# A relational graph convolution: comparison constants in a PSUM bank, and one bank for projections and placement

## The chip, the cores and the metric

The kernel runs on one core of a Trainium2 chip. A core has five engines with a queue each: TensorE (PE in the profile; PEld is its weight load), VectorE (DVE), ScalarE (ACT), GpSimd (POOL) and SyncE (SP). They share the on-chip memory SBUF. TensorE's results land in PSUM, which has 8 banks of 512 float32 columns on each of 128 partitions. The metric is device microseconds of the run, as a median of several runs. One further execution is recorded by the profiler, and all views of the profile are of that one.

## The reference

There are 12500 nodes with 128 features and 200000 edges (src to dst), sorted by dst. An edge's type is the place of the greatest of ten of its attributes. Each layer takes, for every node and type, the mean of the features of the edges' sources, multiplies it by the type's matrix and adds the node's own features times a root matrix and a bias. There are two layers, a relu after the first; then the input is added and each row normalized.

```python
def _rgcn_layer(x, src, dst, edge_type, w_rel, root, bias):
    seg = dst * NUM_REL + edge_type
    sums = segment_sum(x[src], seg); cnt = segment_sum(ones, seg)
    mean = (sums / maximum(cnt, 1.0)[:, None]).reshape(N, NUM_REL, -1)
    return einsum('nrd,rdo->no', mean, w_rel) + x @ root + bias
edge_type = argmax(msg[:, 16:-16], axis=1)
h = relu(_rgcn_layer(x, src, dst, edge_type, w_rel1, root1, b1))
out = layernorm(x + _rgcn_layer(h, src, dst, edge_type, w_rel2, root2, b2))
```

## The kernel before

The edges are cut into 1563 tiles of 128, one edge on each partition, and eight tiles make a group (`G`), 196 groups in a layer. The last group has three tiles. A tile's edges, sorted by destination, reach at most 12 nodes (`WN`), so a pair of type and node within a tile is one of 120 columns (`KW`).

**Preparation** runs by chunks of 128 tiles. `types(c)` loads attributes in two halves and calls `argmax` (L208 to L215): the greatest of ten values (L210), a comparison of all ten with it (L212), a product with descending ranks `riota` (L213), the greatest of these (L214), and the type from it (L215). `count(c)` counts the edges with equal key, and takes a key's neighbours from SBUF and the key itself from a PSUM copy (L309). Both write key, weight and source row per edge (`keyE`, `wE`, `idxE`), via TensorE transposes (L126, L127). Two chunks are prepared ahead of the loop, the others in steps between groups of the first layer.

**The layer loop** takes a group through four stages:

1. `gather` (L404): eight indirect DMAs on GpSimd's queue, each for 128 source rows of 128 float32. The buffers are a ring of 13 groups. All 3126 gathers of the two layers stand on this one queue.
2. `sums`: for each tile, DVE compares the column numbers `iota` with the edge's key and multiplies by its weight (L415, tile `oh`, 128 x 120); once per group it compares `iota` with `place` (L418, tile `at`). TensorE multiplies the rows by `oh` into `zp`, two banks (L421).
3. `project`: ACT copies `zp` to SBUF as `zs` (L436), ten TensorE products with the types' matrices are summed in `po` (L440), and ACT copies that to SBUF as `ms` (L443).
4. `add`: TensorE places `ms` by `at` into 80 node columns (`pa`, L451), and DVE adds these to `acc` (L458).

The loop is software-pipelined: while group g is gathered and summed, g-1 is projected and g-2 added. The order on each engine is made by a scheduler from the dependences, not written by hand. Where a stretch of nodes is complete, `hidden` or `final` finishes its rows (L345 to L395), in pieces of four 128-row tiles.

**PSUM before:** `ps_f` two banks (transposes, counts, root products), `ps_z` two buffers of two banks (`zp`), `ps_o` one bank (`po`), `ps_a` one bank (`pa`). A second path for unusual graphs stands behind a flag (from L551 on) and does not run with these inputs; it calls `argmax` too.

Of the kernel before, what the change touches and what calls it, by code (L numbers as in the profile page):

```python
# [9 lines left out]
F32 = mybir.dt.float32  # L10
# [3 lines left out]
ALU = mybir.AluOpType  # L14
AX = mybir.AxisListType
PSUM = bass.MemoryType.PSUM
# [4 lines left out]
P = 128  # L21
NREL = 10
EMB = 16
RS = 32
WN = 12
KW = NREL * WN
G = 8
QB = 4
SW = 80
# [4 lines left out]
YB = 512  # L34
W = 128
GT = 125
# [5 lines left out]
def rgcn_resnorm_kernel(ctx: ExitStack, tc: tile.TileContext, x, src, dst, attr, w_rel1, root1, b1,  # L42
# [14 lines left out]
    nc = tc.nc  # L57
    N, C = x.shape
    E = src.shape[0]
    D = attr.shape[1]  # L60
# [4 lines left out]
    GR = G * WN  # L65
# [17 lines left out]
    fin = ctx.enter_context(tc.tile_pool(name="fin", bufs=1))  # L83
    small = ctx.enter_context(tc.tile_pool(name="small", bufs=2))
    ps_f = ctx.enter_context(tc.tile_pool(name="ps_f", bufs=2, space=PSUM))

    hD = dram.tile([N, C], F32, name="hD")
    KD = dram.tile([1, L + NT * P + L], F32, name="KD")
# [2 lines left out]
    fast = ctx.enter_context(ExitStack())  # L91
    keep = fast.enter_context(tc.tile_pool(name="keep", bufs=1))
    prep = fast.enter_context(tc.tile_pool(name="prep", bufs=1))
# [4 lines left out]
    spool = fast.enter_context(tc.tile_pool(name="spool", bufs=3))  # L98
    ps_z = fast.enter_context(tc.tile_pool(name="ps_z", bufs=2, space=PSUM))
    ps_o = fast.enter_context(tc.tile_pool(name="ps_o", bufs=1, space=PSUM))  # L100
    ps_a = fast.enter_context(tc.tile_pool(name="ps_a", bufs=1, space=PSUM))

    ident = const.tile([P, P], F32, name="ident")
    make_identity(nc, ident)
# [1 line left out]
    keyE = keep.tile([P, NCH * CT], F32, name="keyE")  # L106
    wE = keep.tile([P, NCH * CT], F32, name="wE")
# [31 lines left out]
    iota = const.tile([P, W], F32, name="iota")  # L139
# [21 lines left out]
                   allow_small_or_imprecise_dtypes=True)  # L161
    riota = const.tile([P, NREL], F32, name="riota")
    nc.vector.tensor_scalar(riota, iota[:, :NREL], -1.0, float(NREL), op0=ALU.mult, op1=ALU.add)
    identb = const.tile([P, P], BF16, name="identb")
    nc.vector.tensor_copy(identb, ident)
    eps = const.tile([P, 1], F32, name="eps")
# [21 lines left out]
    place = keep.tile([GR, NCH * CT // G], F32, name="place")  # L188
# [15 lines left out]
            nc.scalar.dma_start(t, bi.rearrange("(c o) -> c o", o=1))  # L204
            bsb.append(t)

    def argmax(ty, v, p, n, pool):

        top = pool.tile([P, n], F32, name="top")
        nc.vector.tensor_reduce(top[:p], v, axis=AX.X, op=ALU.max)  # L210
        eq = pool.tile([P, n, NREL], F32, name="eq")
        nc.vector.tensor_tensor(eq[:p], v, top[:p, :, None].to_broadcast([p, n, NREL]), op=ALU.is_equal)  # L212
        nc.vector.tensor_tensor(eq[:p], eq[:p], riota[:p, None, :].to_broadcast([p, n, NREL]), op=ALU.mult)  # L213
        nc.vector.tensor_reduce(top[:p], eq[:p], axis=AX.X, op=ALU.max)  # L214
        nc.vector.tensor_scalar(ty, top[:p], -1.0, float(NREL), op0=ALU.mult, op1=ALU.add)  # L215

    def types(c):

        p = chunk_rows(c)
# [27 lines left out]
        for o in (0, H):  # L247
            m = prep.tile([P, H * D], F32, name="m")
            nc.sync.dma_start(m[:n], bass.AP(attr.tensor, attr.offset + (c * CE + o) * D, [[P * D, n], [1, H * D]]))
            if last:  # L250
                nc.sync.dma_start(m[n:p], bass.AP(attr.tensor, attr.offset + (E - P + o) * D,
                                                  [[P * D, 1], [1, H * D]]))
            argmax(ty[:p, o:o + H], m[:p].rearrange("p (j d) -> p j d", d=D)[:, :, EMB:EMB + NREL], p, H, prep)
            yield
        g0 = c * CT // G
        nc.vector.tensor_scalar(bt[:, g0:g0 + ng], bt[:, g0:g0 + ng], 0, N - 1, op0=ALU.max, op1=ALU.min)
# [152 lines left out]
    def sums(table, t0, n):  # L409

        g, gathers = gather(table, t0, n)
        oh = dpool.tile([P, G, KW], F32, name="oh")
        for j in range(n):
            t = t0 + j
            nc.vector.tensor_scalar(oh[:, j, :], iota[:, :KW], keyE[:, t:t + 1], wE[:, t:t + 1], op0=ALU.is_equal,  # L415
                                    op1=ALU.mult)
        at = spool.tile([GR, SW], F32, name="at")
        nc.vector.tensor_scalar(at, iota[:GR, :SW], place[:, t0 // G:t0 // G + 1], None, op0=ALU.is_equal)  # L418
        zp = ps_z.tile([P, G // QB, YB], F32, name="zp")
        for j in reversed(range(n)):  # L420
            m = nc.tensor.matmul(zp[:, j // QB, j % QB * KW:(j % QB + 1) * KW], g[:, j, :], oh[:, j, :],  # L421
                                 start=True, stop=True)
            if j < n - 1:
                tc.keep_in_program_order(m)
                continue

            for d in gathers[:j]:
                tc.add_manual_dep(m.ins, d.ins.name, whole, reason="one wait per group")
        return zp, at

    def project(l, n, zp):

        zs = zpool.tile([P, NREL, G, WN], F32, name="zs")
        for b in range(-(-n // QB)):
            m = min(QB, n - b * QB)
            nc.scalar.activation(zs[:, :, b * QB:b * QB + m, :],  # L436
                                 zp[:, b, :m * KW].rearrange("c (j r n) -> c r j n", r=NREL, n=WN), AF.Copy)
        po = ps_o.tile([P, C], F32, name="po")
        for r in range(NREL):
            nc.tensor.matmul(po[:n * WN], zs[:, r, :n].rearrange("c j n -> c (j n)"), wsb[l][:, r, :],  # L440
                             start=(r == 0), stop=(r == NREL - 1))
        ms = spool.tile([GR, C], F32, name="ms")
        nc.scalar.activation(ms[:n * WN], po[:n * WN], AF.Copy)  # L443
        return ms
# [2 lines left out]

    def add(t0, n, ms, at):

        pa = ps_a.tile([P, SW], F32, name="pa")  # L450
        nc.tensor.matmul(pa, ms[:n * WN], at[:n * WN], start=True, stop=True)  # L451
        if not offs:
            g0 = t0 // G
            offs.extend(nc.values_load_multi_w_load_instructions(
                bt[0:1, g0:min(NG, g0 + 4)], engines=[DVE], min_val=0, max_val=N - 1,
                skip_runtime_bounds_check_because=HELD)[1])
        s = ds(offs.pop(0), SW)
        nc.vector.tensor_tensor(acc[:, s], acc[:, s], pa, op=ALU.add)  # L458
# [90 lines left out]
    def each_tile(before, stages):  # L549

        with tc.For_i(0, E, GT) as e:  # L551
            d_i = gp.tile([P, 1], I32, name="gd_i")
            nc.sync.dma_start(d_i[:GT], dst[ds(e, GT)].rearrange("(e o) -> e o", o=1))
            a = gp.tile([P, 1, D], F32, name="ga")
            nc.sync.dma_start(a[:GT, 0], attr[ds(e, GT), :])
            ty = gp.tile([P, 1], F32, name="gty")
            nc.vector.memset(ty, 0.0)
            argmax(ty[:GT], a[:GT, :, EMB:EMB + NREL], GT, 1, gp)
            d = gp.tile([P, 1], F32, name="gd")
            mx = gp.tile([P, 2], F32, name="gmx")  # L560
            nc.vector.memset(d, -1.0)
            nc.vector.memset(mx[:, 1:2], -float(FAR))
            nc.vector.tensor_copy(d[:GT], d_i[:GT])
            nc.vector.tensor_copy(mx[:, 0:1], d)
            nc.vector.tensor_scalar(mx[:GT, 1:2], d[:GT], -1.0, None, op0=ALU.mult)
            gm = gp.tile([P, 2], F32, name="gm")
            nc.gpsimd.partition_all_reduce(gm, mx, P, bass_isa.ReduceOp.max)
            base = gp.tile([P, 1], F32, name="gbase")
            nc.vector.tensor_scalar(base, gm[:, 1:2], -1.0, 0.0, op0=ALU.mult, op1=ALU.max)
            nc.vector.tensor_scalar(base, base, float(N - 1), None, op0=ALU.min)  # L570
            bw = gp.tile([P, 2], I32, name="gbw")
            nc.vector.tensor_copy(bw[:, 0:1], base)
            nc.vector.tensor_tensor(d, d, base, op=ALU.subtract)
            span = gp.tile([P, 1], F32, name="gspan")
            nc.vector.tensor_tensor(span, gm[:, 0:1], base, op=ALU.subtract)
            nc.vector.tensor_scalar(span, span, 0.0, float(N - 1), op0=ALU.max, op1=ALU.min)
            nc.vector.tensor_copy(bw[:, 1:2], span)
            nc.vector.tensor_scalar(bw[:, 1:2], bw[:, 1:2], 7, None, op0=ALU.arith_shift_right)
            nc.vector.tensor_scalar(bw[:, 1:2], bw[:, 1:2], 1.0, None, op0=ALU.add)
            state = before(e, ty)  # L580
            nw = nc.values_load(bw[0:1, 1:2], min_val=1, max_val=-(-N // W), skip_runtime_bounds_check_because=HELD)
            b0 = nc.values_load(bw[0:1, 0:1], engines=[DVE, SP], min_val=0, max_val=N - 1,
                                skip_runtime_bounds_check_because=HELD)
            for body, after in stages:
                dw = gp.tile([P, 1], F32, name="gdw")
                nc.vector.tensor_copy(dw, d)
                with tc.For_i(0, nw, 1) as k:
                    body(dw, state, window(b0, k))
                    nc.vector.tensor_scalar(dw, dw, -float(W), None, op0=ALU.add)
                if after:  # L590
                    state = after(state)
# [101 lines left out]
```

## Time and profile before

| | us |
|---|---|
| median of 3 runs | 4721.93 (4706.83 to 4728.79) |
| profiled execution | 4026.78 |
| its span, first to last instruction | 4025.1 |
| GpSimd busy | 3023.0 |
| TensorE busy | 2499.6 |
| VectorE busy | 1345.0 |
| ScalarE busy | 566.0 |
| mean granted TensorE clock | 0.82 of full |

A row of the page's list of groups names line, engine, operation and tiles (out<-in), how often it ran, its busy time and mean duration, and then how long the engine stood idle just before it, with what ended most of that. In the chain of waits, "issue" is time in which an engine waited for nothing that the profile shows. A timeline row is a start, a duration, the engine and its instructions, merged where they follow each other. The profiled execution is 695 us shorter than the median of the runs.

### The profile page before, as it was taken

The numbers are of one execution on the slowest core, as the hardware profiler recorded it, in microseconds if no ns is written. First come the engines' busy times: TensorE is split into PE (matmuls) and PEld (weight loads), VectorE is DVE, ScalarE is ACT, GpSimd is POOL, SyncE is SP. The second block draws the span as 40 slices with busy tenths as digits, with TensorE's granted clock in tenths as the row PEclk, the third lists the DMA queues.
The fourth block names the chain that finished last, engine by engine and source line by source line (L and its number), as shares of the span: only waits on it lengthen the run. The fifth ranks groups of instructions, "written<-read, shape, count | busy, mean of one in ns | idle before, by whom it ended". The sixth has DMA issues, their size and how long they took to land.

```text
span 4025.1 us, 45940 instructions
## 1 busy us (share of the span) xinstructions
PE 2499.6 (62%) x16184; PEld 2382.6 (59%) x16184; DVE 1345.0 (33%) x4911; ACT 566.0 (14%) x1293; POOL 3023.0 (75%) x3142
## 2 busy tenths in 40 slices
PE   3666665656666666666555656666656666666666
PEld 2656565656556566655555656566656656665665
DVE  7443343334334333322222322223222322232222
ACT  0111111111111111111111111111111111111111
POOL 7777777777777777777767777777777777777775
PEclk9887888887888888788878887877888888878878
DMA  5332233233222222222222222222222222222222
GB/s 175 119 94 76 73 88 87 64 87 86 59 64 64 59 58 58 63 58 58 56 59 57 65 61 60 60 61 68 61 60 61 68 61 60 61 68 60 60 61 56
DMA packets 180736, 279.13 MB, mean 69 GB/s; under 512 B 55793, under 2 KB 127360, under 8 KB 177376
## 3 DMA queue, kind: packets, MB, share of 16 engines
q0 software_dynamic: 100032, 205.07, 20.2%
q1 hardware_dynamic: 77302, 69.59, 5.5%
q8 instruction: 136, 2.23, 0.2%
q10 hardware_dynamic: 3168, 1.44, 0.1%
q14 instruction: 98, 0.80, 0.1%
HBM read 262.28 MB, written 13.60 MB: 69 GB/s over the span
## 4 chain that ended last, share of the span: by engine, by line
POOL 61%; issue 28%; PE 6%; DMA 5%; DVE 0%; ACT 0%; POOLq 0%; ACTq 0%
POOL g L404 61%; DMA g<-in_x_dram,idxE 2%; PE zp L421 2%; DMA g<-hD,idxE 2%; PE po L440 2%; PE pf L355 1%; PE pf L356 1%; PE pf L350 0%; PE pa L451 0%; DVE acc L506 0%; DMA s_i<-in_src_dram 0%; DMA hD<-hb 0%; ACT ms L443 0%; POOLq L404 0%; DVE acc L458 0%
## 5 line engine op out<-in xcount | busy, mean ns | idle before, releaser
L421 PE MATMUL zp<-oh,g 128*128 128x120 f32 x6252 | 1207.7, 373 | 1445.8 <-DMA g<-in_x_dram,idxE 700.3
L421 PEld LDWEIGHTS zp<-oh,g 128*128 128x128 f32 x6252 | 1126.3, 279 | 1530.9 <-issue 1512.7
L404 POOL DMA_INDIRECT g<-in_x_dram,idxE x1563 | 1521.9, 974 | 482.4 <-issue 464.5
L404 POOL DMA_INDIRECT g<-hD,idxE x1563 | 1498.9, 959 | 495.5 <-issue 464.7
L415 DVE TENSOR_SCALAR oh<-iota,keyE,wE 128x120 f32<-128x120 f32 x3126 | 858.6, 346 | 1905.3 <-PE zp L421 1905.2
L440 PE MATMUL po<-w,zs 128*96 128x128 f32 x7840 | 1068.8, 297 | 0.6 <-ACT zs L436 0.6
L440 PEld LDWEIGHTS po<-w,zs 128*96 128x96 f32 x7840 | 1018.7, 185 | 1.5 <-ACT zs L436 0.9
L436 ACT ACTIVATE zs<-zp 128x480 f32<-128x480 f32 (+1 forms) x782 | 403.4, 567 | 2599.8 <-PE zp L421 2576.7
L458 DVE TENSOR_TENSOR acc<-acc,pa 128x80 f32 x392 | 93.0, 237 | 651.1 <-PE pa L451 641.0
L443 ACT ACTIVATE ms<-po 96x128 f32<-96x128 f32 x392 | 106.9, 273 | 703.5 <-PE po L440 703.2
L451 PE MATMUL pa<-at,ms 96*128 96x80 f32 (+1 forms) x784 | 184.2, 329 | 1.6 <-ACT ms L443 1.4
L451 PEld LDWEIGHTS pa<-at,ms 96*128 96x128 f32 (+1 forms) x784 | 172.9, 271 | 2.8 <-ACT ms L443 2.8
L418 DVE TENSOR_SCALAR at<-iota,place 96x80 f32<-96x80 f32 x392 | 107.1, 273 | 0.0
L309 DVE TENSOR_TENSOR eqb<-pf,kh 128x1344 bf16<-128x1344 f32 (+1 forms) x65 | 100.2, 1549 | 14.5 <-PE pf L313 13.9
L355 PE MATMUL pf<-root,fT 128*128 128x128 f32 x392 | 79.2, 284 | 0.7 <-DMA g<-hD,idxE 0.7
L356 PE MATMUL pf<-ident,a 128*128 128x128 f32 x392 | 76.1, 276 | 0.4 <-DVE a L345 0.4
L355 PEld LDWEIGHTS pf<-root,fT 128*128 128x128 f32 x392 | 59.6, 192 | 5.3 <-ACT fT L352 4.7
L356 PEld LDWEIGHTS pf<-ident,a 128*128 128x128 f32 x392 | 59.4, 192 | 1.3 <-DVE a L345 1.0
L311 PE MATMUL pf<-eqb,identb 128*128 128x512 bf16 (+1 forms) x130 | 50.0, 384 | 16.4 <-DVE eqb L309 16.4
L313 PE MATMUL pf<-eqb,identb 128*128 128x512 bf16 (+1 forms) x130 | 50.2, 386 | 0.0
L352 ACT ACTIVATE fT<-pf 128x512 f32<-128x512 f32 (+2 forms) x52 | 29.9, 575 | 11.3 <-PE pf L350 6.6
L313 PEld LDWEIGHTS <-identb 128*128 128x128 bf16 (+1 forms) x130 | 12.7, 97 | 26.6 <-issue 18.4
(96 smaller groups left out, 462.7 us busy)
## 6 DMA issues: line engine op xcount, KB each, us to landing
m<-in_edge_attr_dram SPq DMA_DIRECT2D x24, 1344.0 KB
g<-in_x_dram,idxE POOLq DMA_INDIRECT x1563
g<-hD,idxE POOLq DMA_INDIRECT x1563
xb<-in_x_dram SPq DMA_DIRECT2D x48, 256.0 KB
hD<-hb SPq DMA_DIRECT2D x24, 256.0 KB
hb<-hD SPq DMA_DIRECT2D x24, 256.0 KB
out_dram<-o SPq DMA_DIRECT2D x24, 256.0 KB
w<-in_L_gnn_w_rel_dram ACTq DMA_DIRECT2D x2, 640.0 KB
```

The source lines that it names most:

```text
L309: nc.vector.tensor_tensor(eq[:p], kp[:p, None, :R].to_broadcast([p, DB, R]), ahead, op=ALU.is_equal)
L355: nc.tensor.matmul(pr[:h, t, :], fT[:, t * P:t * P + h], rsb[l], start=True, stop=False)
L356: nc.tensor.matmul(pr[:h, t, :], a[:, t * P:t * P + h], ident, start=False, stop=True)
L404: return g, [nc.gpsimd.indirect_dma_start(out=g[:, j, :], out_offset=None, in_=table, in_offset=(bass.IndirectOffsetOnAxis(ap=idxE[:, t0 + ...
L415: nc.vector.tensor_scalar(oh[:, j, :], iota[:, :KW], keyE[:, t:t + 1], wE[:, t:t + 1], op0=ALU.is_equal, op1=ALU.mult)
L418: nc.vector.tensor_scalar(at, iota[:GR, :SW], place[:, t0 // G:t0 // G + 1], None, op0=ALU.is_equal)
L421: m = nc.tensor.matmul(zp[:, j // QB, j % QB * KW:(j % QB + 1) * KW], g[:, j, :], oh[:, j, :], start=True, stop=True)
L436: nc.scalar.activation(zs[:, :, b * QB:b * QB + m, :], zp[:, b, :m * KW].rearrange("c (j r n) -> c r j n", r=NREL, n=WN), AF.Copy)
L440: nc.tensor.matmul(po[:n * WN], zs[:, r, :n].rearrange("c j n -> c (j n)"), wsb[l][:, r, :], start=(r == 0), stop=(r == NREL - 1))
L443: nc.scalar.activation(ms[:n * WN], po[:n * WN], AF.Copy)
L451: nc.tensor.matmul(pa, ms[:n * WN], at[:n * WN], start=True, stop=True)
L458: nc.vector.tensor_tensor(acc[:, s], acc[:, s], pa, op=ALU.add)
```

## The change

A new pool `ps_c` holds one PSUM bank for the whole kernel. Into it go a copy of the column numbers (`iotaP`, 120 columns), a copy of the ranks (`riotaP`) and two places of 64 columns for the maxima in `argmax` (`topP`), one for each half of a chunk. `oh` and `at` are then compared from `iotaP`, and `argmax` uses `riotaP` and `topP`. Their outputs stay in SBUF, except the maxima. The path behind the flag still passes SBUF tiles. To make room, `ps_a` is dropped: `po` and `pa` become two uses of one tile name `pp` in `ps_o`, which has one buffer, so each waits until the other has been read.

In the order that the scheduler makes of it, ten `po` products, the placement `pa` and the next `po` still alternate. In the second layer's steady stretch two products of the next `zp` now stand between `pa` and `po`, and six behind `po`; DVE's `oh` of one group stand between two additions, one group less ahead than before. The gathers keep their order and their waits.

```diff
+    ps_c = ctx.enter_context(tc.tile_pool(name="ps_c", bufs=1, space=PSUM))
...
-    ps_a = fast.enter_context(tc.tile_pool(name="ps_a", bufs=1, space=PSUM))
...
+    bank = ps_c.tile([P, YB], F32, name="bank")
+    iotaP = bank[:, :KW]
+    riotaP = bank[:, P:P + NREL]
+    topP = [bank[:, (3 + k) * P // 2:(4 + k) * P // 2] for k in range(2)]
+    nc.vector.tensor_copy(iotaP, iota[:, :KW])
+    nc.vector.tensor_copy(riotaP, riota)
...
-    def argmax(ty, v, p, n, pool):
-        top = pool.tile([P, n], F32, name="top")
+    def argmax(ty, v, p, n, pool, ri, top):
         nc.vector.tensor_reduce(top[:p], v, axis=AX.X, op=ALU.max)
...
-        nc.vector.tensor_tensor(eq[:p], eq[:p], riota[:p, None, :].to_broadcast([p, n, NREL]), op=ALU.mult)
+        nc.vector.tensor_tensor(eq[:p], eq[:p], ri[:p, None, :].to_broadcast([p, n, NREL]), op=ALU.mult)
...
-            argmax(ty[:p, o:o + H], m[:p].rearrange("p (j d) -> p j d", d=D)[:, :, EMB:EMB + NREL], p, H, prep)
+            argmax(ty[:p, o:o + H], m[:p].rearrange("p (j d) -> p j d", d=D)[:, :, EMB:EMB + NREL], p, H, prep,
+                   riotaP, topP[o // H])
...
-            nc.vector.tensor_scalar(oh[:, j, :], iota[:, :KW], keyE[:, t:t + 1], wE[:, t:t + 1], op0=ALU.is_equal,
+            nc.vector.tensor_scalar(oh[:, j, :], iotaP, keyE[:, t:t + 1], wE[:, t:t + 1], op0=ALU.is_equal,
                                     op1=ALU.mult)
...
-        nc.vector.tensor_scalar(at, iota[:GR, :SW], place[:, t0 // G:t0 // G + 1], None, op0=ALU.is_equal)
+        nc.vector.tensor_scalar(at, iotaP[:GR, :SW], place[:, t0 // G:t0 // G + 1], None, op0=ALU.is_equal)
...
-        po = ps_o.tile([P, C], F32, name="po")
+        po = ps_o.tile([P, C], F32, name="pp")
...
-        pa = ps_a.tile([P, SW], F32, name="pa")
+        pa = ps_o.tile([P, C], F32, name="pp")[:, :SW]
```

More of the change, by code (lines that the diff above doesn't have):

```diff
@@ L557, in each_tile @@
             nc.vector.memset(ty, 0.0)
-            argmax(ty[:GT], a[:GT, :, EMB:EMB + NREL], GT, 1, gp)
+            argmax(ty[:GT], a[:GT, :, EMB:EMB + NREL], GT, 1, gp, riota,
+                   gp.tile([P, 1], F32, name="gtop"))
             d = gp.tile([P, 1], F32, name="gd")
```

## The prediction

> **What bounds the kernel now.** I read the page first, then the waits, then the DVE rows with their forms kept apart, then the timeline at a few places.
>
> ```profile
> span 4025.1 us, 45940 instructions
> PE 2499.6 (62%) x16184; PEld 2382.6 (59%) x16184; DVE 1345.0 (33%) x4911; ACT 566.0 (14%) x1293; POOL 3023.0 (75%) x3142
> ...
> POOL 61%; issue 28%; PE 6%; DMA 5%; DVE 0%; ACT 0%; POOLq 0%; ACTq 0%
> ...
> L404 POOL DMA_INDIRECT g<-in_x_dram,idxE x1563 | 1521.9, 974 | 482.4 <-issue 464.5
> L404 POOL DMA_INDIRECT g<-hD,idxE x1563 | 1498.9, 959 | 495.5 <-issue 464.7
> L415 DVE TENSOR_SCALAR oh<-iota,keyE,wE 128x120 f32<-128x120 f32 x3126 | 858.6, 346 | 1905.3 <-PE zp L421 1905.2
> ```
>
> The chain that ended last is 61% POOL and 28% "issue": GpSimd works through 3126 gathers one behind another, and between two of them it waits for nothing that the profile shows. 465/1563 gives 0.30 us of such pause per gather. An undisturbed gather takes 0.94 us (below), so its step is 1.245 us and a group of eight is 9.96 us. 3126 x 1.245 = 3892; the first gather starts at 9.3 us, the second layer's first one waits 20 us for its table, and some 24 us follow the last one: 3945. The span has 80 us more. Those sit in the means of the two gather rows: 974 and 959 ns instead of about 943. (974 - 943) x 1563 + (959 - 943) x 1563 = 48 + 25 = **73 us**. The timeline shows what lengthens a gather:
>
> ```profile
> 1115.59 1.08 POOL L404 DMA_INDIRECT g<-in_x_dram,idxE  x1 [0.30 <-issue]
> 1116.97 2.05 POOL L404 DMA_INDIRECT g<-in_x_dram,idxE  x1 [0.31 <-issue]
> 1119.33 0.94 POOL L404 DMA_INDIRECT g<-in_x_dram,idxE  x1 [0.30 <-issue]
> 1120.58 1.53 POOL L404 DMA_INDIRECT g<-in_x_dram,idxE  x1 [0.30 <-issue]
> ...
> 1115.68 1.59 DVE L415 TENSOR_SCALAR oh<-iota,keyE,wE 128x120 f32<-128x120 f32 x6
> 1117.19 0.81 DVE L212 TENSOR_TENSOR eq<-m,top 128x640 f32<-128x640 f32 x1
> ...
> 1119.00 1.56 DVE L309 TENSOR_TENSOR eqb<-pf,kh 128x1344 bf16<-128x1344 f32 x1 [0.79 <-PE pf L313]
> 1120.48 0.81 DVE L213 TENSOR_TENSOR eq<-eq,riota 128x640 f32<-128x640 f32 x1
> ```
>
> A gather beside the oh comparisons takes 1.08, beside L212 and L213 (both inputs in SBUF) 2.05 and 1.53. Beside L309, a longer comparison of the same kind, it takes 0.94. L309 has one input in a PSUM tile (pf). So DVE delays GpSimd by how it reads SBUF, and one operand in PSUM ends that. Going through the trace's gathers one by one: the 54 beside L309 alone have a mean of 943.8 ns. 574 last over 950 ns, 70.8 us over 944 together: 41.3 us in 446 gathers beside L415 or L418, 8.4 in 52 beside these and another DVE operation, 18.7 in 41 beside L212 or L213, 2.5 in others.
>
> **The change part by part.**
>
> *oh and at from PSUM.* L309 says that the delay goes. I take all of the 41.3 us and some 6 of the 8.4 (L345, L347 and L395 keep their SBUF operands): **-47 us**, all on GpSimd's chain.
>
> *The argmax.* L212 and L213 get one PSUM input: **-19 us**. Here a rule of the Trainium skill speaks against the change: "SBUF - State Buffer", section "Who interferes with whom", says of tensor_tensor that it takes only the read side of the port that DVE and GpSimd share, and infers that descriptor generation, which needs the write side, isn't stalled. By the rule this part is worth 0 and the sum is -47; by the rows (2.05 and 1.53 us) it is -66. I take the rows: these gathers also read their row numbers from SBUF.
>
> *Price on DVE.* From SBUF, these operations run at two columns per cycle. Rows with forms apart:
>
> ```profile
> L418 DVE TENSOR_SCALAR at<-iota,place 96x80 f32<-96x80 f32 x392 | 107.1, 273 | 0.0
> L127 DVE COPY wE<-pf 128x128 f32<-128x128 f32 x12 | 3.5, 288 | 10.8 <-PE pf L126 10.8
> L134 DVE CAST s_f<-s_i 128x128 f32<-128x128 int32 x12 | 2.6, 219 | 0.2 <-DMA s_i<-in_src_dram 0.2
> ```
>
> 128 columns out of PSUM take 288 ns, out of SBUF 219: 69 more. L385's 512 columns in 691 ns against 291 for 128 make 1.04 ns per column at single rate, so 64 columns are 67 ns: the slower rate explains all of the 69, the fixed part is the same. For oh's 120 columns I take +65 ns, for at +43: 3126 x 65 + 392 x 43 = 203 + 17 = 220 us of DVE time; argmax 0, as its comparisons run at single rate already (L212: 812 ns for 640). Gained back: 256 of the oh took over 400 ns (mean 486 against 332), waiting for GpSimd: -39. DVE goes from 33 to about 38%. In a steady group it is busy 2.94 us of 10:
>
> ```profile
> 2600.00:3100.00 500.00, 310.60 (x1987) 300.78 (x1986) 145.44 (x580) 69.24 (x160) 379.51 (x396) 0.81 0.24 62
> ```
>
> (columns: length, then PE, PEld, DVE, ACT, POOL busy, clock, DMA share, GB/s.) It becomes 3.5. Cover: oh has to be ready before its zp. In the built order the oh are queued one group ahead of the acc addition's reach in place of two, so 10 us of cover remain for 2.7 us of work. On the path: **0**. Without the cover it would be 0.5 us per group, 205 us.
>
> *The start.* Two copies to PSUM (L163's small one 107 ns, a wide one some 280) enter DVE's queue ahead of the first gather, which waited 6.3 us for DVE: **+0.4 us**.
>
> *pa and po in one bank.* Before, po of the next group starts while DVE reads pa. Now po waits until acc has been added: PE waits, and behind po stand six of the next zp and all later groups. Price: the addition follows pa by some 0.04 us, runs 0.24 and needs about as long again to release: 0.35 us, x 391 = 137 us of PE time if nothing covers it; up to 2.5 us per group if the addition stands behind a burst of eight oh (8 x 0.315), below 0 not at all, as a wait only is added. "Perfetto Trace Analysis", section "Matmuls", of the Trainium skill warns of just this: independent groups should rotate through banks so that emptying one overlaps the next one's matmuls. By the rule: +137 us, a sum of +71. The rows: PE is busy 311 of 500 us, 6.2 us of a group's 10, and each zp burst comes after some 4 us in which PE waits for the gathers. The built order also puts two zp matmuls (8 took 2.6 us, so 0.65) between pa and po. I take **0**, and keep +137 for the range. GpSimd would notice PE only if it fell behind by the ring of 13 groups, 130 us.
>
> **Sum:** -47 - 19 + 0.4 = -66 us: a span of 3959, -1.6%.
>
> **From the profiled execution to the median.** It took 4026.8 us, the runs 4721.9: 695 us more, and no view shows where. If they are something that the change doesn't touch, 4722 - 66 = 4656; if everything scales, 4722 x 3959/4025 = **4645**. I take the second; between them lie 0.2%.
>
> **Rivals.**
> *B, the 695 us are this delay too.* Per group they are 1.78 us, and a burst of eight oh and an at lasts 2.3 us: were GpSimd shut out for most of each burst when nothing records, the runs would drop to about 4722 - 695 - 66 = 3961. For it: nothing else on the chain could be so elastic. Against it: in the trace GpSimd slips in between two oh, a beside-oh gather loses 93 ns on average (41.3/446), rarely over 170. Two such delays of 170 ns in every burst would be 391 x 0.34 = 133 us, 83 more than now: 4560. So B lies between 3960 and 4550.
> *C, the delay stays.* oh keeps two SBUF operands, the scalars keyE and wE, and writes to SBUF; L309 has no such scalars. Then only the argmax part comes: 4722 - 19 = 4703, no change that can be measured (0.5%, 24 us, is about what this kernel's measurement tells from nothing). Against it: L261, out of PSUM with a scalar from SBUF, left its gathers at 943 to 947, but few.
> *D, slower: the shared bank makes PE the bound.* Place: po behind the acc addition. A matmul of po starts 110 ns after the last one where the full clock is granted and 213 where half is (the clock of 0.81 is a mix of the two). All at half: 38 matmul passes x 0.213 = 8.1 us per group; +0.35 and a burst of oh of 2.5 in front of the addition = 10.95. It decides from 9.96 on: 391 x 10.95 + 54 = 4335, +7.7%, so 5086 in runs. For it: the runs are slow for a reason unseen, and PE at half clock would be near the bound. Against it: it needs the clock and the queue both at their worst.
>
> **How the numbers follow.** A (4645) 0.50, B 0.24, C 0.10, D 0.16. Faster by over 0.5%: A and B, 0.74; within: C, 0.10; slower: D, 0.16. A's own range is 4560 (all bursts unlucky) to 4690 (half the saving). To leave out no more than 0.2, D and the lowest sixth of B stay out: 4000 to 4745.
>
> **What would show it.** Right: gathers at 943 to 948 ns in both layers and none near 2 us; L415 at about 395 ns with no tail over 500; DVE near 1530 us; PE waiting for DVE's addition without GpSimd ever waiting for PE; a span near 3960. If the gathers stay at 959 and 974, C; if they shorten and the runs fall by far more than the profile, B; if POOL waits for PE's zp, D. The prediction fails if the runs' unseen 695 us move either way.

## The result, and the profile after

| | us |
|---|---|
| before, median of 11 runs | 4726.63 (4706.83 to 4752.11) |
| after, median of 11 runs | 4748.16 (4731.54 to 4756.81) |
| ratio | 1.0040, 95% interval 1.0025 to 1.0055 |
| profiled execution of after (one of the 11), its span | 4748.3 |

The forecast was 4645 us, with a range of 4000 to 4745. The change does not make the kernel faster: the time after lies 0.4% above the time before. These lines are of the page of after: its span, the busy times, the shares of the chain of waits, and rows of its list of groups (busy, mean ns | idle time before, and what ended most of it).

```profile
span 4748.3 us, 46227 instructions
PE 2639.3 (56%) x16184; PEld 2450.8 (52%) x16184; DVE 1500.8 (32%) x4913; ACT 549.2 (12%) x1293; POOL 2961.3 (62%) x3142
...
another core or an unknown queue 48%; PE 29%; issue 12%; ACT 4%; DVE 4%; POOL 2%; DMA 1%; ACTq 0%; DVEq 0%; SPq 0%; POOLq 0%
...
L411 POOL DMA_INDIRECT g<-hD,idxE x1563 | 1479.2, 946 | 871.7 <-issue 423.8
L411 POOL DMA_INDIRECT g<-in_x_dram,idxE x1563 | 1479.8, 947 | 840.6 <-issue 426.6
...
L422 DVE TENSOR_SCALAR oh<-bank,keyE,wE 128x120 f32<-128x120 f32 x3126 | 1013.1, 388 | 20.0 <-PE zp L428 18.8
...
L450 ACT ACTIVATE ms<-pp 96x128 f32<-96x128 f32 x392 | 106.7, 272 | 2548.2 <-remote 1546.5
```

Read first what came as forecast. The gathers last 946 and 947 ns in place of 959 and 974: their delay is nearly gone in both layers. Gather by gather, what lies over 944 ns in those above 950 fell from 70.8 us to 10.3, and most of that rest stands beside operations whose inputs the change leaves in SBUF (L289, L352, L402). An oh lasts 388 ns (395 were forecast), and DVE is busy 1500.8 us (about 1530).

Now what did not. GpSimd, 75% busy in the profile of before, is 62% busy, and its idle time before gathers has grown from some 490 to over 840 us in each layer. It has 2% of the chain instead of 61%; 48% goes to "another core or an unknown queue", and ACT's row says "remote". Only one core runs here. An engine or a DMA tells the others that its work is done by updating a semaphore, a counter on which they wait. The labels stand where the trace holds such an update, but no instruction that ended in the 1.5 us before it and could have made it. In the page of before, the same copy was released by PE:

```profile
L443 ACT ACTIVATE ms<-po 96x128 f32<-96x128 f32 x392 | 106.9, 273 | 703.5 <-PE po L440 703.2
```

So the saved 62 us of gather time (3020.8 to 2959.0) went into a longer wait of GpSimd. GpSimd's waits, by what ended them (us in total, times, longest):

```profile
POOL g L411 <- issue: 850.3, 2777, 3.3
POOL g L411 <- remote: 471.9, 231, 18.4
POOL g L411 <- PE zp L428: 272.5, 58, 8.0
```

In the profile of before no gather waits for a zp. A place in after's timeline shows who is waiting (start, duration, engine and instructions):

```profile
3006.47 2.42 PE L447 MATMUL pp<-w,zs 128*96 128x128 f32 x20 [2.10 <-issue]
...
3008.73 1.27 PE L428 MATMUL zp<-oh,g 128*128 128x120 f32 x10
...
3015.09 0.94 POOL L411 DMA_INDIRECT g<-hD,idxE  x1 [0.30 <-issue]
3019.01 0.27 ACT L450 ACTIVATE ms<-pp 96x128 f32<-96x128 f32 x1 [11.79 <-remote]
...
3019.31 0.94 POOL L411 DMA_INDIRECT g<-hD,idxE  x1 [3.27 <-remote]
3019.33 0.72 PE L458 MATMUL pp<-at,ms 96*128 96x80 f32 x2 [6.57 <-ACT ms L450]
```

The last po product ends at 3008.9. ACT, which has nothing else to do, copies it at 3019.01, ten us later; PE, which waits for the copy, then places ms, and GpSimd too starts again 0.3 us after the copy began. ACT is not at fault: the trace has an update of PE's semaphore at 3018.93, 82 ns before the copy. In the profile of before the update stands 14 ns behind the end of the last product (median), and the copy starts 82 ns behind the update there too. PE's ends are modelled, but PE itself goes on to the next zp at 3008.73. I call this a **late announcement**: the work is done, and the semaphore tells of it later. In the profile of before every one of the 392 ms copies starts within 0.4 us of the last product; in after 193 start over 1 us late, 1557 us together, and 164 of these start within 0.12 us of an update of PE's semaphore. Whether the change brings this, or the timed executions of before had it too, was the first thing to test.

### The profile page after: what moved, and what is told of

It reads as the page before. It is cut to its first block, busy times and chain, and to the rows that moved or that the text cites. A ratio compares the mean times of both kernels' runs of the same rounds, so it can differ in the third digit from the quotient of the medians.

```text
span 4748.3 us, 46227 instructions
## 1 busy us (share of the span) xinstructions
PE 2639.3 (56%) x16184; PEld 2450.8 (52%) x16184; DVE 1500.8 (32%) x4913; ACT 549.2 (12%) x1293; POOL 2961.3 (62%) x3142
## 4 chain that ended last, share of the span: by engine, by line
another core or an unknown queue 48%; PE 29%; issue 12%; ACT 4%; DVE 4%; POOL 2%; DMA 1%; ACTq 0%; DVEq 0%; SPq 0%; POOLq 0%
PE pp L447 14%; PE zp L428 10%; ACT zs L443 3%; PE pp L458 3%; DVE oh L422 2%; POOL g L411 2%; ACT ms L450 1%; PE pf L363 1%; PE pf L362 1%; DMA g<-in_x_dram,idxE 0%; DVE eqb L316 0%; PE pf L320 0%; DVE acc L465 0%; PE pf L357 0%
## 5 line engine op out<-in xcount | busy, mean ns | idle before, releaser
L447 PE MATMUL pp<-w,zs 128*96 128x128 f32 x7840 | 1333.7, 341 | 657.6 <-issue 407.4
L447 PEld LDWEIGHTS pp<-w,zs 128*96 128x96 f32 x7840 | 1250.8, 218 | 713.0 <-issue 435.8
L428 PE MATMUL zp<-oh,g 128*128 128x120 f32 x6252 | 1048.2, 313 | 356.2 <-issue 333.8
L428 PEld LDWEIGHTS zp<-oh,g 128*128 128x128 f32 x6252 | 940.9, 226 | 367.1 <-issue 350.4
L422 DVE TENSOR_SCALAR oh<-bank,keyE,wE 128x120 f32<-128x120 f32 x3126 | 1013.1, 388 | 20.0 <-PE zp L428 18.8
L465 DVE TENSOR_TENSOR acc<-acc,pp 128x80 f32 x392 | 92.5, 236 | 2807.2 <-PE pp L458 1609.3
L458 PE MATMUL pp<-at,ms 96*128 96x80 f32 (+1 forms) x784 | 199.4, 345 | 964.1 <-ACT ms L450 817.2
L458 PEld LDWEIGHTS pp<-at,ms 96*128 96x128 f32 (+1 forms) x784 | 151.4, 241 | 1059.5 <-ACT ms L450 903.7
L450 ACT ACTIVATE ms<-pp 96x128 f32<-96x128 f32 x392 | 106.7, 272 | 2548.2 <-remote 1546.5
L425 DVE TENSOR_SCALAR at<-bank,place 96x80 f32<-96x80 f32 x392 | 113.5, 290 | 0.3 <-issue 0.3
```

What stands on the lines that cost most here:

```text
L422: nc.vector.tensor_scalar(oh[:, j, :], iotaP, keyE[:, t:t + 1], wE[:, t:t + 1], op0=ALU.is_equal, op1=ALU.mult)
L425: nc.vector.tensor_scalar(at, iotaP[:GR, :SW], place[:, t0 // G:t0 // G + 1], None, op0=ALU.is_equal)
```

## The experiments

Each set of runs was made on one chip, together with the kernel before. In four of the five sets below that took 4723.66 to 4778.92 us; in the last it took 4025.37. For the first runs, two theories of the 695 us that the profile of before did not show: **P**, announcements of TensorE's results are late and the loop over the groups is the bound; **G**, the gathers are held up more than in the profile, by DVE.

**First set (before: 4723.66 us, 31 runs). The kernel before, recorded once more.** No edit.

> The kernel before once more, unchanged, for a second profile of it. Theory P (the engine that ends last in the runs is TensorE: its results are announced late to ACT and DVE, as in the profile after, and the first profile of before was an execution without that): span near 4720, copies of po starting up to 10 us after the last po product in about half of the groups, GpSimd idle well over the 0.30 us per gather. Theory G (GpSimd's gathers are held up by DVE in the runs): span near 4720 with gathers of a mean near 1.17 us and none waiting for TensorE; or the profile shows 4026 again.

Measured 4722.79 us. Lines of its page:

```profile
span 4721.1 us, 45940 instructions
...
another core or an unknown queue 41%; PE 35%; issue 12%; POOL 7%; ACT 4%; DMA 0%; DVE 0%; ACTq 0%; POOLq 0%; DVEq 0%; SPq 0%
...
L404 POOL DMA_INDIRECT g<-hD,idxE x1563 | 1501.1, 960 | 858.0 <-issue 426.0
L404 POOL DMA_INDIRECT g<-in_x_dram,idxE x1563 | 1525.9, 976 | 758.1 <-issue 425.5
```

The gathers last as long as in the first profile of before (960 and 976 ns), but GpSimd idles 1616 us before them in place of 978, and has 7% of the chain. 202 ms copies are over 1 us late. So the 695 us are not GpSimd's: G falls, and the profile that the prediction stands on is of an execution with another bound than the timed ones. Counting tiles shows it as well: at 3019 us GpSimd has begun 2021 gathers and zp 1923 tiles, twelve groups apart with a ring of 13; at the same time of the first profile they are 1.2 groups apart. Nor are the transfers slower: from the start of a gather to the last of its 16 small packets (the DMA records, in order of time) it takes 2.20 us here and 2.22 us in the first profile (medians). In 188 of the 202 late copies an update of PE's semaphore stands within 0.12 us before the start. Of the gathers' own semaphores this trace has 12,341 updates, the first one 49,948.

**po and pa in one bank, alone.**

```diff
-    ps_a = fast.enter_context(tc.tile_pool(name="ps_a", bufs=1, space=PSUM))
...
-        po = ps_o.tile([P, C], F32, name="po")
+        po = ps_o.tile([P, C], F32, name="pp")
...
-        pa = ps_a.tile([P, SW], F32, name="pa")
+        pa = ps_o.tile([P, C], F32, name="pp")[:, :SW]
```

> Before, with po and pa in one bank and nothing else changed (one PSUM bank stays unused). Theory P: TensorE is the bound in the runs, so the wait for the addition is paid: 4740 to 4780, most of what the whole change cost or more. Theory G: the shared bank is covered, 4727 within 0.5%.

Measured 4726.9 us, 1.0008 (0.9999 to 1.0016). The shared bank costs at most some 8 us, though in the profile PE waits 173.7 us before po products for the addition. By its number this is theory G's case; theory P's 4740 to 4780 missed.

**The change with oh and at from SBUF**: argmax from the PSUM bank, po and pa sharing.

```diff
-            nc.vector.tensor_scalar(oh[:, j, :], iotaP, keyE[:, t:t + 1], ...
+            nc.vector.tensor_scalar(oh[:, j, :], iota[:, :KW], keyE[:, t:t + 1], ...
...
```

> The change, but with oh and at compared from the column numbers in SBUF as before; argmax uses the PSUM bank, po and pa share theirs. Theory P: as the shared bank alone, within 10 us of it, since 19 us less on GpSimd's gathers buys nothing where GpSimd waits for TensorE. Theory G: 4727 - 19 = 4708.

Measured 4721.96 us, 0.9998 (0.9984 to 1.0012): nothing, as theory P had it; theory G's 4708 missed.

**Second set (before: 4728.17 us, 31 runs). The change with the argmax from SBUF.**

```diff
...
-                   riotaP, topP[o // H])
+                   riota, prep.tile([P, H], F32, name="top"))
```

> The change, with argmax as before (ranks and maxima in SBUF); oh and at still come from PSUM, po and pa still share a bank. The argmax alone and the shared bank alone were each worth nothing (4721.96 and 4726.9 us), the whole change 20 to 25. Theory D (the longer oh, 388 us in place of some 340 ns, delays what DVE does between TensorE's steps): the whole +20 to +25 us is here, 4740 to 4750. Theory S (several small costs add, none by itself): 4725 to 4735.

Measured 4725.75 us, 0.9996 (0.9982 to 1.0011). Theory D missed. The time lies at the foot of theory S's 4725 to 4735, but beside its own kernel before that is no cost: neither this nor the other parts tried carries the 0.4%.

**Wider oh in SBUF.** The kernel before, with 200 columns:

```diff
-        oh = dpool.tile([P, G, KW], F32, name="oh")
+        oh = dpool.tile([P, G, KW + 80], F32, name="oh")
...
-            nc.vector.tensor_scalar(oh[:, j, :], iota[:, :KW], keyE[:, t:t + 1], ...
+            nc.vector.tensor_scalar(oh[:, j, :], iota2, keyE[:, t:t + 1], ...
...
```

> The kernel before, with oh compared over 200 columns in SBUF in place of 120 (the last 80 are not used), two banks for po and pa, argmax as before. At the double rate of SBUF 80 columns more are some 42 ns per oh, two thirds of what PSUM costs. Theory D (the time of DVE counts, wherever it comes from): +12 to +20 us, 4735 to 4745. Theory B (the read of the PSUM bank itself disturbs TensorE's work in PSUM): no change, 4720 to 4727, except for gathers held up longer by SBUF reads, which have slack in these executions.

Measured 4749.11 us, 1.0043 (1.0030 to 1.0055): just above theory D's times, and not theory B's. Two rows of its page:

```profile
L407 POOL DMA_INDIRECT g<-hD,idxE x1563 | 1641.4, 1050 | 735.4 <-issue 444.1
L407 POOL DMA_INDIRECT g<-in_x_dram,idxE x1563 | 1666.8, 1066 | 657.9 <-issue 431.8
```

GpSimd is busy 281 us more than in the second profile of before, as longer reads of SBUF hold its gathers longer, and DVE 134 us more; the time rises by 21 us. Most of what either engine has more of does not reach the end in these executions; which of the two the 21 us come from, this run can't say.

**Two of ten products.** The kernel before, with types 0 and 9 alone in the projection:

```diff
-        for r in range(NREL):
+        for r in (0, NREL - 1):
```

> The kernel before, with two of the ten products in each projection (types 0 and 9 only); gathers, oh, zp, copies, placement and additions are as before. 6272 products of some 160 ns net to 327 ns as recorded go. Theory P (TensorE with its late announcements sets the end in the timed runs, GpSimd has slack): the time falls by some 600 to 750 us, to where GpSimd's queue of gathers bounds it at 3950 to 4100. Theory G (GpSimd's queue sets the end in the timed runs too, at a longer step): within 1% of 4722.

Measured 4628.84 us, 0.9793 (0.9749 to 0.9837), from two runs. PE's po row shrinks from 1251.1 to 382.9 us and the time by 99. P as I had put it, TensorE as the bound, is wrong, and G's number within 1% is missed too: 123 ms copies are still over 1 us late, and GpSimd idles 1554 us before its gathers.

**Half of the gathers.** The kernel before; each pair of tiles uses the rows of its first:

```diff
-            ... for j in range(n)]
+            ... for j in range(0, n, 2)]
...
-            m = nc.tensor.matmul(zp[...], g[:, j, :], oh[:, j, :],
+            m = nc.tensor.matmul(zp[...], g[:, j // 2 * 2, :], oh[:, j, :],
...
```

> The kernel before, with every second gather left out: the tiles of a pair are summed from the rows of the first. TensorE, DVE and ACT have as much to do as before. Theory P with its cause in the gathers (N: announcements are late because the gathers' own notices come ahead of them): half the notices, so half or more of the late announcements go and the time falls to 3000 to 3900. Theory P with its cause in TensorE itself: no gather bounds it, the time stays at 4600 to 4722. Theory G: falls to TensorE's own work, 2700 to 3000, with no late announcements left to see.

Measured 2608.09 us, 0.5518 (0.5496 to 0.5540), from two runs, and below what any of the three theories gave. Lines of its page:

```profile
PE 2055.6 (79%) x16184; PEld 1967.3 (75%) x16184; DVE 1332.2 (51%) x4911; ACT 559.9 (21%) x1293; POOL 1552.0 (60%) x1580
...
PE 70%; another core or an unknown queue 14%; issue 8%; ACT 4%; DVE 3%; DMA 1%; SPq 0%; POOL 0%; ACTq 0%; DVEq 0%; POOLq 0%
```

2120 us go with 1562 gathers, 1.36 us for each, though GpSimd had idled a third of its time. PE now has 70% of the chain; the ms copies that are over 1 us late are late by 635 us together, in the second profile of before by 2310. So most of the lateness goes with the gathers, and since the busiest engine worked 64% of the second profile of before, no engine's own work explains the 4722.

**Third set (before: 4778.80 us, 24 runs). A ring of 4 groups** in place of 13, to see whether running far ahead is what makes announcements late.

```diff
-RING = 13
+RING = 4
```

> The kernel before with a ring of 4 groups of gather buffers in place of 13, nothing else. In the second profile of before GpSimd runs some 10 to 12 groups ahead of zp, in the first 1.2. Theory R (being far ahead is itself what makes the announcements late, through a long list of gathers not yet taken): with 4 groups ahead at most, the lateness goes with it, 4030 to 4200. Theory N (announcements are served at a limited rate, and each gather brings as many as before): the number of gathers is unchanged, so 4700 to 4760. Theory P' (the loop over the groups needs the reserve to ride over late announcements): slower, 4800 to 5200.

Measured 4740.98 us, 0.9929 (0.9907 to 0.9951). The time lies among N's, which were set down for a kernel before of 4727 us; R's 4030 to 4200 are far off. 221 ms copies are over 1 us late: the reserve isn't the cause.

**The whole change again.**

> The whole change again, on the chip of the other three of this call. The runs of its parts gave 0.9998 (argmax alone), 0.9996 (oh and at alone) and 1.0008 (shared bank alone), the whole 1.0040. If the cost is real and lies in the parts together: 1.003 to 1.005 again. If 1.004 was a matter of the chip or the session: 0.999 to 1.001.

Measured 4784.78 us, 1.0021 (1.0006 to 1.0036): between the two cases.

**Gathers of 64 rows.**

```diff
-            out=g[:, j, :], ... ap=idxE[:, t0 + j:t0 + j + 1]
+            out=g[:P // 2, j, :], ... ap=idxE[:P // 2, t0 + j:t0 + j + 1]
...
```

> The kernel before with gathers of 64 rows in place of 128 (the edges on partitions 64 to 127 are left out of the sums); as many gathers, as many notices of them, half the rows and bytes, and the same number of TensorE instructions. Leaving out every second gather gave 2608 us. Theory N (what counts is how many gathers are announced): 4600 to 4722. Theory D2 (what counts is the rows that a gather fetches, by its descriptors or its GpSimd time): 2600 to 3300.

Measured 4756.97 us, 0.9970 (0.9951 to 0.9990). Half the rows and bytes save 0.3%; half the gathers saved 45%. By the ratio this is N's case. It is the number of gathers that counts, and not what each brings. The run can't part their announcements from GpSimd's own work on a gather, as that hardly depends on the rows (925 and 943 ns in place of 960 and 976), nor from the number of transfers: a gather still makes 16 packets of data, half as large.

**Fourth set (before: 4778.92 us, 21 runs). A small DMA for every gather**, on SP's queue.

```diff
...
+        for j in range(n):
+            tiny = tpool.tile([1, 16], F32, name="tiny")
+            nc.sync.dma_start(tiny, x[t0 + j:t0 + j + 1, :16])
```

> The kernel before, with one DMA of 64 bytes on SP's queue added for every gather (3126 of them, into tiles that nobody reads), so that the number of DMAs that announce themselves doubles while GpSimd has nothing more to do. Theory N (announcements of all kinds are served at a limited rate, and the DMAs' own make up nearly all of them): a large rise, 5500 us or more, unless one small DMA brings far fewer than a gather does, then at least 100 us. Theory Q (it is GpSimd's own work on a gather that keeps other engines' announcements waiting, whatever the DMA brings): within 0.5% of before.

Measured 4783.03 us, 1.0006 (0.9992 to 1.0020), as theory Q had it. A small DMA brings one packet of 4 bytes, a gather 16 (the DMA records: 3126 more such packets on SP's queue, 50016 on the gathers'), so this adds about 6% of such packets, not the double that the expectation names first. Its condition for that case, at least 100 us, isn't met. A limit on announcements in general is unlikely by that; one on the gathers' 16 is still possible.

**A ring of 2 groups.**

> The kernel before with a ring of 2 groups of gather buffers. A ring of 4 gave 0.9929 of before. If announcements are late by what GpSimd has still before it, less reserve means shorter delays, and the loss of overlap counts less than that: 0.98 to 0.99. If 4 groups were already what a steady chain needs: 1.00 to 1.06, because a gather then waits for the zp of the group before the last.

Measured 4740.49 us, 0.9913 (0.9888 to 0.9939): just outside the first case, and about the same as with 4.

**The whole change with a ring of 4.**

> The whole change with a ring of 4 groups. If the ring's gain and the change's cost stand beside each other: 0.993 x 1.003 = 0.996 of before. If the change costs only where GpSimd is 10 to 12 groups ahead and DVE is queued by that: 0.993.

Measured 4754.17 us, 0.9941 (0.9920 to 0.9962); the interval holds both cases.

**oh and at from PSUM, argmax as before, again.**

> The change with the argmax as before, on another chip and with more runs: it gave 0.9996, the whole change 1.0040 and 1.0021. If the cost is that of DVE's longer comparisons (about a tenth of 156 us of DVE time, as with the wide oh in SBUF, 131 us and 20 us): 1.002 to 1.004. If the first value stands, the cost needs the argmax part beside it: 0.999 to 1.001.

Measured 4745.06 us, 0.9929 (0.9911 to 0.9947): neither case, and not the 0.9996 of the same kernel two sets earlier. Differences of up to 0.7% between kernels do not carry over from one set to another here, though the interval within a set is 0.2% wide.

**Fifth set (before: 4025.37 us, 17 runs, 4020.00 to 4029.78).** The chip of this set runs the kernel before as in the first profile. **The same kernel a third time:**

> The change with the argmax as before, for the third time. It gave 0.9996 where the kernel before took 4728 us and 0.9929 where it took 4779. If the ratio follows the chip on which it runs: one of these two again, by the time of before. If it wanders between calls: anything from 0.99 to 1.00, and differences of this size between kernels are not to be put down to their edits.

Measured 3978.33 us (3975.32 to 3981.39), 0.9885 (0.9870 to 0.9900): 47.0 us less, and below all that was expected. Its page:

```profile
span 3974.8 us, 46221 instructions
...
POOL 62%; issue 28%; DMA 7%; PE 2%; DVE 0%; POOLq 0%; ACT 0%; ACTq 0%; DVEq 0%
...
L408 POOL DMA_INDIRECT g<-in_x_dram,idxE x1563 | 1491.6, 954 | 481.7 <-issue 456.8
L408 POOL DMA_INDIRECT g<-hD,idxE x1563 | 1475.6, 944 | 495.6 <-issue 460.5
...
L419 DVE TENSOR_SCALAR oh<-bank,keyE,wE 128x120 f32<-128x120 f32 x3126 | 1022.4, 389 | 18.0 <-PE zp L425 18.0
```

GpSimd's chain is back (62% and 28%), its idle time is "issue" alone, no ms copy is late. The gathers are 53.6 us shorter in sum than in the first profile of before, and here the time follows. The second layer's have no delay left; the first layer's 954 keep what L212 and L213 do to them. In the second and fourth set the same kernel shortened the gathers nearly as much (955 and 945, 956 and 947 ns) and the time by 0.04 and 0.7%.

**A ring of 2 again.**

> The kernel before with a ring of 2 groups, on another chip and with more runs. It gave 0.9913, a ring of 4 gave 0.9929. If the gain is the ring's: 0.990 to 0.994. If it was a matter of the chip, where the kernel before took 4779 us and not 4727: 0.998 to 1.002.

Measured 4075.23 us, 1.0124 (1.0108 to 1.0139): slower here by 50 us. One line of its waits says where:

```profile
POOL g L404 <- PE zp L421: 49.5, 1, 49.5
```

It is a single wait, at the start: the preparation lets the first zp begin only after some 76 us, and with two groups of buffers GpSimd has by then stood still for 50 of them. With 13 it gathers more than six groups meanwhile. In the fourth set a ring of 2 has the same wait (48.8 us), and its time was 38 us below that of before: there GpSimd had the slack for it. Neither case of the expectation holds.

**A ring of 2 with oh and at from PSUM.**

> A ring of 2 groups with oh and at from PSUM and the argmax as before. If both add: 0.985 to 0.99. If either only removes the same waiting: 0.991 to 0.993. If both were matters of the chip: 0.998 to 1.002.

Measured 4028.40 us, 1.0007 (0.9999 to 1.0015): the ring's +50 and the oh's -47 add up, as they should where one queue is the bound.

**The queue filled up.** Half of the gathers, and a GpSimd instruction in place of each one left out:

```diff
+            nc.gpsimd.iota(fill, pattern=[[1, 1200]], base=0, ...)
...
```

> The kernel with every second gather left out (2608 us), and in the place of each left-out gather a GpSimd instruction that numbers 1200 columns in SBUF, an estimated 1.1 to 1.3 us from the 234 ns of 128 columns and 158 ns of 41: GpSimd's queue is about as long as before (some 3900 us), half of its gathers are gone. Theory Q (announcements are late while GpSimd works, on whatever): 4500 to 4750, GpSimd idle at the heads of groups as before. Theory H (only the gathers make them late, by what they do beyond GpSimd's own time): GpSimd's queue itself is the bound, 3850 to 4050, and few ms copies are late.

Measured 3610.33 us, 0.8970 (0.8953 to 0.8986). Neither theory gave this, and it can't answer its question, as it came to the set in which before has no late announcements. What it shows is another thing:

```profile
L421 DVE TENSOR_SCALAR oh<-iota,keyE,wE 128x120 f32<-128x120 f32 x3126 | 2352.7, 1304 | 543.8 <-PE zp L427 543.0
L409 POOL IOTA fill<- 128x1200 f32 x1564 | 1799.4, 1151 | 10.8
```

An oh takes 1304 ns in place of some 345. The 2227 of them that overlap an iota take 1690 ns on average, the other 899 take 349: DVE's comparison from SBUF is held while GpSimd writes SBUF. The delay between the two engines goes both ways.

## Why the prediction was wrong

*What bounds the kernel now.* Right for the execution that was recorded, and for the fifth set of runs; wrong for the runs whose median was to be forecast. There the loop over the groups, held up by late announcements, is the bound, and GpSimd waits for it.

*oh and at from PSUM (-47).* Right in mechanism and size where GpSimd is the bound: 47.0 us (interval 40 to 52) in the fifth set, with the shared bank beside it. The gathers beside oh or at, which lost 49.7 us in the first profile of before, lost 3.9 there. In the others the same microseconds came off the gathers and went into GpSimd's waits.

*The argmax (-19).* Of its cause the runs show this: over 944 ns, the gathers that overlap L212 or L213 (by their numbers in before) lost 18.7 us in the first profile of before, 12 to 15 in the profiles with oh in PSUM and the argmax in SBUF (second, fourth and fifth set), and 0.2 in after. So these operations do hold gathers up, and one operand in PSUM ends it, as the prediction read from the rows, but it is worth some 12.5 us beside the oh in PSUM rather than 19. That is against the inference in "SBUF - State Buffer", "Who interferes with whom", of the Trainium skill, that tensor_tensor does not stall descriptor generation; the same section's statement that two SBUF inputs contend with a GpSimd instruction that reads SBUF agrees with it. The gather of 2.05 us among the prediction's lines overlaps L282 too (0.28 us, two SBUF inputs), so not all of its delay is L212's. What the argmax is worth in time was not measured where it could count: the whole change had no run in the fifth set. From the 4025.4 of before there, less 47 and 12.5, it would be some 3966 us, an estimate.

*Price on DVE (+65 per oh, 0 on the path).* The size is about right: 388 and 389 ns in place of 395, and +17 ns for an at in place of +43, so DVE is busy 156 us more in place of the 181 net. On the path it was 0 in the fifth set. In the others it can't be told apart from the scatter between sets.

*The start (+0.4).* Too small to be seen in the time; the first gather waits 5.6 us for DVE in after, 6.3 in before.

*pa and po in one bank (0).* Right: 1.0008 (0.9999 to 1.0016) alone, at most 8 us; and in the fifth set PE waits 8.5 us in all before po products for the addition, and 23.8 before their weight loads. The +137 us, which the prediction set down by the rule on rotating banks ("Perfetto Trace Analysis", "Matmuls", of the Trainium skill), did not reach the time: not in the fifth set, where PE stands idle before most bursts of zp, and not in the first, where PE waited 173.7 us at the bank.

*From the profiled execution to the median.* **This step failed.** It says: "695 us more, and no view shows where. If they are something that the change doesn't touch, 4722 - 66 = 4656; if everything scales, ... 4645." Both cases let the saving through, and so take for granted that the same queue ends last in executions that are 17% longer. The third case, that the 695 us are a different bound, under which GpSimd has slack and its saving is worth nothing, is not among the rivals: B made the 695 us GpSimd's delay, C kept the delay, D put PE's clock and a wait at the shared bank in its place. D was nearest in seeing the loop over the groups as the bound, but gave it a price of its own, 5086, and blamed the change's wait for it; nor does the time follow TensorE's clock: the granted clock was 0.73 in before, 0.75 with the shared bank alone, at the same time, and 0.63 with two of the ten products, at 2.1% less. C's 4703 lies nearest to the measured time, but by luck: C kept the delay of the gathers, and that went. The profile gave no reason why each step of the queue should last 0.22 us longer (695/3126) in the timed runs. That the queue would wait instead was the other reading, and it wasn't weighed.

What stays open. Why PE's semaphore is updated late on some chips and prompt on another: the runs show that it goes with the number of gathers (half of them: -45%), and neither with their rows (-0.3%), the ring (-0.7 and -0.9%), nor eight tenths of the projections' work (-2.1%). In after 158 of the 193 late ms copies start in or just behind a pause of GpSimd of over 1 us, pauses that are 17% of its time. That fits announcements that get through when GpSimd pauses, but also pauses that end by the same announcement. Whether the difference belongs to a chip or to a condition that outlasts a set of runs isn't known. A rival that no run here tests is the recording: every run on record carries a span and a clock, so all were recorded in some form, and the long executions have only about a quarter of the gathers' semaphore updates in their traces. Whether those are lost, or several updates are made at once, is not known. And the change's +0.4 and +0.2% have no cause: the parts tried gave none, and kernels wander by 0.7% between sets. That it is a real cost of the whole change was not shown.

## What to carry to other kernels

When the profiled execution and the timed ones differ by more than the change is worth, record the kernel again until both agree, before any sum is made: here one more profile would have shown that the queue with all the saving had 638 us more of idle time. An engine's time counts only in executions where the others wait for it; look at who waits for whom there, and not at its share of busy time. Where a wait ends later than the work it waits for, compare three times: the end of the work, the update of its semaphore, and the start of the waiter. And a gain of under 1% measured in one set of runs should be seen in a second one, on another chip, with the same sign.

## What the hardware showed that I had not expected

- The same kernel takes 4025 us in one set of runs and 4724 to 4779 in the others, each within 1% inside its set. The parting sign in the trace is the time from the last product of a projection to the copy that waits for it: at most 0.4 us in the one, over 1 us for about half of the groups in the others (202 of 392 in the second profile of before). It is PE's semaphore that is updated late; the copy follows its update by the same 82 ns.
- There, with half of the gathers left out, each one saved 1.36 us of the time, though it lasts 0.96 us; half the rows and bytes of all of them save 0.3%.
- An oh that overlaps GpSimd's 1200-column iota takes 1690 ns on average, the others 349.
